# Macaron block on one core: side steps of attention ordered behind the main matmul stream

## The chip, the cores and the metric

The kernel runs on one core of one Trainium2 chip. The metric is the device time of one execution in microseconds (us), lower is better. Three runs of the kernel before took 1823.98 to 1827.08 us, median 1824.61 us.

## The reference, cut to what matters

The input x has 4096 tokens of 256 numbers. It goes through half a feed-forward network, an attention and a second half of the same network, each behind a layer norm:

```python
x = x + 0.5 * ffn(layernorm(x))
x = x + attn(layernorm(x))
x = x + 0.5 * ffn(layernorm(x))
```

The network has a shared part, `silu(x @ sg) * (x @ su) @ sd` with an inner width of 2048, and 8 experts with an inner width of 1024. A router picks two experts for each token, an expert takes at most 640 tokens, and its result is added with the router's weight. Attention works within groups of 64 tokens: q, k, v = x @ w_qkv, q and k pass an RMS norm with weights ln_w, there are 16 heads of 16 numbers, scores are masked causally, and after the softmax comes a product with w_proj. All is float32.

## The kernel before, in words

Every float32 matmul is made of three float16 matmuls: each operand is split into a high part and a low part (high x high, high x low, low x high; `TERMS`, L35). `split` (L102) does this for weights: ScalarE writes the high part (L105), VectorE the low part (L106).

There are four stages (L788 to L817). Stage a does router and shared network of the first half for token blocks 0 to 3; stage b its experts; stage c the shared network of blocks 4 to 7 of the first half, the attention, and the shared network of blocks 0 to 6 of the second half; stage d the experts of the second half and its last shared block. A block is 512 tokens.

The main stream of a shared block (`shared`, L380) runs over 16 chunks of 128 inner columns. For each, `gate_up` (L327) makes two products on TensorE (`pgu`, 6 matmuls of 512 columns each, L337). In stage c the first is followed by tanh on ScalarE (L344) and a VectorE product (L345) that together give silu. After the second, VectorE multiplies both (L350, called the product here), ScalarE casts the high part `hh` (L352) and VectorE subtracts to the low part `hl` (L353). Then `down` (L356) multiplies both by sdw into two PSUM banks `po` (L361, 12 matmuls of 256 columns). The down of a chunk is deferred (`defer`, L97): it is traced after the next chunk's gate and up. After chunk 15 the two banks are evicted into the residual (L394, `xr`) and stored (L397). As its down is deferred, this is traced after the first gate and up of the next block, and the next block's down needs the same two banks. The residual is loaded at chunk 2 (`res_load`, L371). The `pgu` tiles share three PSUM banks; attention and router share three others in stages a and c (`ps_m`, L90).

`shared` yields three times a chunk: after the gate, after the up, after the deferred down. `drive` (L716) mixes the side work in at these points. Every `RATE_C` = 3 main steps it makes one slot of tile steps (`Tiles.steps`, L686) and traces two steps at each following main step, and the rest at the end of the slot; at the end of a block it traces the open slot out. In stage c a side tile is 128 tokens of attention and the next router (`attn_tile`, L507, then `front_steps`, L640, and for each fourth tile `route`, L226), about 27 steps long; a new one starts every `GAP_C` = 4 slots, oldest first within a slot. By steps: load y (L512), stats, normed and cast (L160, L169, L170), transpose by DMA (L179), products `pqk` and `pv` with squares and `vs` (L528 to L541), scaling (L545) and the `QK` copies (L555 to L563), transposes (L567), scores `psc` and mask (L575, L578), maximum and copies of V (L583, L588), exp (L592 to L595), transpose (L598), `py` and `Y` (L606 to L614), a second load of y and the split of Y (L617, L170), transposes (L624), `pao` and the addition (L629, L630), then the norm, transposes and logits of the second half.

What sets the order on each engine: the program is traced in the order above, and then a scheduler orders each engine's queue at build time. It goes through the program with a model of durations, takes from what the model says is ready the instruction that was traced earliest, and so lets a side step overtake the main stream wherever the model finds its input ready. On the chip each queue then runs in that order. `issue_after(ins)` forbids this for a block of code: each of its instructions on the engine of `ins` is queued behind `ins`. It adds no wait. `behind` (L192) applies it to `self.latest`, of which entry 0 is the last ScalarE lookup and entry 1 the last VectorE product. Stage a's tiles are already held so (`Tiles(tile1, 32, GAP_A, n)`, L794); in stage c they are not, and the tanh path of `gate_up` leaves entry 0 as it was.

`attn_init` (L472) runs ahead of stage c's first block. It loads w_qkv in four pieces (L480, one buffer) and w_proj in two pieces of eight loads (L486, one buffer), and splits each piece at once. `fed` (L702) feeds a generator of weights beside a main stream; stage a uses it for the shared weights, once every six main steps.

Of the kernel before, what the change touches and what calls it, by code (L numbers as in the profile page):

```python
# [8 lines left out]
F32 = mybir.dt.float32  # L9
# [5 lines left out]
AF = mybir.ActivationFunctionType  # L15
ALU = mybir.AluOpType
# [4 lines left out]
P = 128  # L21
H = 256
# [3 lines left out]
WS = 16.0  # L26
XP = UP * WS
# [10 lines left out]
class Net:  # L38
# [288 lines left out]
    def gate_up(self, wc, x, h, tanh=False):  # L327

        nc = self.nc
        n = x.shape[-1]  # L330
        ps = []
        for i in range(2):
            p = self.ps_gu.tile([P, n], F32, name="pgu", tag="gu")
            j = 0
            for k in range(2):
                for (w, a) in TERMS:
                    nc.tensor.matmul(  # L337
                        p, lhsT=wc[:, w, i, k, :], rhs=x[:, 2 * a + k, :], start=(j == 0), stop=(j == 5))
                    j += 1
            ps.append(p)  # L340
            if i == 0:
                s = self.hp.tile([P, BT], F32, name="sl", bufs=self.nsl)[:, :n]
                if tanh:
                    nc.scalar.activation(s, p, AF.Tanh, scale=0.5 / XP)  # L344
                    nc.vector.scalar_tensor_tensor(  # L345
                        out=s, in0=s, scalar=1.0, in1=p, op0=ALU.add, op1=ALU.mult)
# [3 lines left out]
        self.latest[1] = nc.vector.scalar_tensor_tensor(  # L350
            out=s, in0=ps[1], scalar=1.0 / XP / (2.0 * XP if tanh else 1.0), in1=s, op0=ALU.mult, op1=ALU.mult).ins
        nc.scalar.copy(h[0], s)  # L352
        nc.vector.tensor_tensor(out=h[1], in0=s, in1=h[0], op=ALU.subtract)  # L353
        yield

    def down(self, outs, nt, h, wd, c, nch):  # L356
# [23 lines left out]
    def shared(self, b, xb, src, dst, tanh=False, late=2):  # L380
        nc = self.nc
        outs = [self.ps_out.tile([P, BT], F32, name="po", tag="po") for _ in range(2)]
        for c in range(16):
            if c == late:
                res = self.res_load(src, b)
            h = [a[:, 0:BT] for a in self.hbuf()]
            yield from self.gate_up(self.sgu[:, c], xb, h, tanh)

            def fin(c=c, h=h):
                self.down(outs, 4, h, self.sdw[:, :, c], c, 16)  # L390
                if c < 15:
                    return
                for i in range(2):
                    nc.vector.scalar_tensor_tensor(  # L394
                        out=res[i], in0=outs[i].rearrange("p (t f) -> p t f", f=H), scalar=0.5 / WS,
                        in1=res[i], op0=ALU.mult, op1=ALU.add)
# [72 lines left out]
            for _ in nxt:  # L469
                pass  # L470

    def attn_init(self, w_qkv, ln_w, w_proj):  # L472
        nc = self.nc
        a = self.at
        self.wqkv = a.tile([P, 2, 2, 3 * H], F16, name="wqkv")
        self.wpr = a.tile([P, 2, 2, H], F16, name="wpr")
        for k in range(2):
            for c0, n in ((0, 2 * H), (2 * H, H)):
                r = a.tile([P, 2 * H], F32, name="rq", tag="q32")[:, :n]
                nc.sync.dma_start(out=r, in_=w_qkv[k * P:(k + 1) * P, c0:c0 + n])  # L480
                self.split(self.wqkv[:, 0, k, c0:c0 + n], self.wqkv[:, 1, k, c0:c0 + n], r)
        wp = w_proj.rearrange("(j r c) f -> r j c f", r=2, c=16)
        for k in range(2):
            r = a.tile([P, H], F32, name="rp", tag="yy")
            for j in range(8):
                nc.sync.dma_start(out=r[j * 16:(j + 1) * 16], in_=wp[k, j])  # L486
            self.split(self.wpr[:, 0, k], self.wpr[:, 1, k], r)
        self.lnw = a.tile([P, H], F32, name="lnw")
        nc.sync.dma_start(out=self.lnw, in_=ln_w.unsqueeze(0).to_broadcast([P, H]))
        self.mask = a.tile([P, 64], F32, name="mask")  # L490
        m2 = self.sm.tile([P, 64], F32, name="m2", bufs=1)
        for m, base in ((self.mask, 0), (m2, -64)):
            nc.gpsimd.memset(m, 0.0)
            nc.gpsimd.affine_select(
                out=m, in_=m, pattern=[[-1, 64]], compare_op=ALU.is_ge, fill=-3.0e38,
                base=base, channel_multiplier=1)
        nc.vector.tensor_copy(self.mask[64:P], m2[64:P])
        self.QK = a.tile([P, 24, P], F16, name="QK")
# [200 lines left out]
        self.slot += 1  # L699


def fed(main, weights):  # L702

    for i, _ in enumerate(main):
        if i % 6 == 0:
            next(weights, None)
        yield

# [27 lines left out]
def macaron(ctx, tc, x, w_qkv, ln_w, w_proj, router_w, rg, ru, rd, sg, su, sd, out):  # L736
    nc = tc.nc
    x = x.rearrange("b s h -> (b s) h")
    out = out.rearrange("b s h -> (b s) h")
    n = Net(ctx, tc)  # L740
    R1 = n.route_init(0)
# [42 lines left out]
    def all_shared(key, b, src, dst, **k):  # L784
        yield from n.shared(b, fbs[key]["xb"], src, dst, **k)
        used.add(key)

    with n.phase("a", BT, 2, 16):  # L788
        n.ident = n.at.tile([P, P], F32, name="ident")
        make_identity(nc, n.ident)  # L790
        weights = n.load_shared(sg, su, sd)
        next(weights)
        n.load_router(router_w)
        tiles = Tiles(tile1, 32, GAP_A, n)  # L794
        run_slots(tiles, ready(1, 0))
# [62 lines left out]
```

## Time and profile before

| | |
|---|---|
| three runs, median (lowest to highest) | 1824.61 us (1823.98 to 1827.08) |
| profiled execution, and its span | 1828.36 us, 1826.6 us |
| TensorE clock granted, mean | 0.998 |
| stage c | about 604 to 1440 us |
| first attention weight split, first `pqk` | 617.5 us, 632.3 us |
| main block ends in stage c, from L394's starts | 682.3, 760.2, 840.7, 921.8, 1002.5, 1083.3, 1164.0, 1244.7, 1318.9, 1388.4 us |
| busy in 720 to 834 us (114 us): PE, DVE, ACT, POOL | 114.0, 89.5, 75.6, 73.4 us |
| busy in 834 to 846 us (12 us): PE, DVE, ACT, POOL | 10.4, 9.5, 8.4, 6.9 us |
| DMA share of 720 to 834, and of 834 to 846 us | 0.67, 0.83 |

PE is TensorE's matmuls, PEld its weight loads, DVE VectorE, ACT ScalarE, POOL GpSimd, SP SyncE, which issues DMAs here. A line of a timeline gives the start in us, the length in us, engine, line, operation, output<-inputs, shapes and how many were merged; in brackets stands how long the engine had been idle before it and what ended that. The waits view sums such idle times by the waiting line and by what ended them. A busy TensorE is not TensorE at its peak, since its matmuls overlap and their ends are modelled.

### The profile page before, as it was taken

To read this page: it belongs to the slowest core of one execution; us is meant where nothing else is said; L and a number is where in the kernel's file an instruction comes from. 1 tells how busy PE (TensorE), PEld (TensorE's weight loads), DVE (VectorE), ACT (ScalarE), POOL (GpSimd) and SP (SyncE) were. 2 spreads that over 40 slices of the span, in tenths; PEclk is the share of its full clock that TensorE was granted. 3 is DMA by queue.
4 is the path that set the end of the run, shared out by engine and by line. 5 is a ranking of instruction groups with operands and counts; after the bars stand their busy time and mean duration, and the time that the engine had idled before them with its cause. 6 is when DMAs were issued, how large, how long until landed. Compare 5 with 4: busy or idle time off the path is not lost.

```text
span 1826.6 us, 37514 instructions
## 1 busy us (share of the span) xinstructions
PE 1778.0 (97%) x13724; PEld 1197.1 (66%) x13724; DVE 1198.9 (66%) x2891; ACT 951.6 (52%) x2055; POOL 754.5 (41%) x1072
## 2 busy tenths in 40 slices
PE   6999999999999899999999999999999999999998
PEld 3555657777777556666666666666655677777765
DVE  6665545666666567787777877887756566666643
ACT  4433334555555466666666666666333455555542
POOL 4666630122111334566767676776430011113210
PEclk9999999999999999999999999999999999999999
DMA  6244132455443356767576776756213144455420
GB/s 196 80 114 114 32 88 63 108 125 120 115 108 87 83 82 99 134 111 148 118 144 118 133 146 117 144 100 130 51 28 73 32 111 108 111 122 122 102 44 12
DMA packets 439193, 185.95 MB, mean 102 GB/s; under 512 B 302305, under 2 KB 436125, under 8 KB 439008
## 3 DMA queue, kind: packets, MB, share of 16 engines
q1 hardware_dynamic: 420528, 161.60, 40.8%
q0 software_dynamic: 17664, 21.17, 6.5%
q8 instruction: 107, 1.75, 0.4%
q10 hardware_dynamic: 816, 0.79, 0.1%
q14 instruction: 78, 0.64, 0.1%
HBM read 78.95 MB, written 42.21 MB: 66 GB/s over the span
## 4 chain that ended last, share of the span: by engine, by line
PE 47%; issue 21%; POOL 12%; DVE 10%; DMA 5%; ACT 3%; SPq 1%; another core or an unknown queue 1%; POOLq 0%; DVEq 0%; ACTq 0%
PE pgu L337 29%; PE po L361 15%; POOL xg L318 3%; DVE sl L350 2%; DMA acc<-eo,eidscatter 2%; DVE sl L345 1%; DVE hl L353 1%; POOL X L316 1%; POOL rstd L150 1%; POOL acc L460 1%; PE pqk L637 1%; POOL S L584 1%; POOL xa L170 1%; ACT sl L344 1%
## 5 line engine op out<-in xcount | busy, mean ns | idle before, releaser
L337 PE MATMUL pgu<-xb,sgu 128*128 128x512 f16 x3072 | 742.2, 380 | 15.5 <-DVE sl L345 8.6
L352 ACT CAST hh<-sl 128x512 f16<-128x512 f32 (+2 forms) x512 | 273.1, 534 | 481.5 <-DVE sl L350 465.5
L337 PE MATMUL pgu<-xe,wc 128*128 128x384 f16 (+1 forms) x3072 | 497.0, 299 | 0.0
L337 PEld LDWEIGHTS <-sgu 128*128 128x128 f16 x3072 | 293.4, 98 | 291.7 <-issue 24.2
L350 DVE SCALAR_TENSOR_TENSOR sl<-pgu,sl 128x512 f32<-128x512 f32 (+2 forms) x512 | 300.7, 588 | 244.8 <-PE pgu L337 213.3
L353 DVE TENSOR_TENSOR hl<-sl,hh 128x512 f16<-128x512 f32 (+2 forms) x512 | 310.8, 607 | 152.6 <-ACT hh L352 147.2
L361 PEld LDWEIGHTS <-hh 128*128 128x128 f16 x3328 | 320.8, 98 | 107.9 <-ACT hh L352 7.3
L337 PEld LDWEIGHTS <-wc 128*128 128x128 f16 x3072 | 300.6, 98 | 92.0
L361 PE MATMUL po<-sdw,hh 128*128 128x256 f16 x2048 | 350.0, 273 | 3.4 <-ACT hh L352 2.2
L361 PE MATMUL po<-sdw,hl 128*128 128x256 f16 x1024 | 247.6, 273 | 6.6 <-DVE hl L353 5.9
L361 PE MATMUL po<-wd,hh 128*128 128x256 f16 x1280 | 223.6, 273 | 0.0
L460 POOL DMA_INDIRECT out_dram<-eo,eidscatter x40 | 65.2, 1629 | 341.5 <-DVE eo L459 331.8
L348 ACT ACTIVATE sl<-pgu 128x384 f32<-128x384 f32 (+1 forms) x336 | 158.9, 473 | 73.0 <-PE pgu L337 43.8
L361 PEld LDWEIGHTS <-hl 128*128 128x128 f16 x1664 | 162.8, 98 | 48.5 <-DVE hl L353 14.7
L460 POOL DMA_INDIRECT acc<-eo,eidscatter x40 | 66.2, 1655 | 293.4 <-DVE eo L459 283.7
L318 POOL DMA_INDIRECT xg<-X,di x128 | 131.3, 1026 | 54.8 <-issue 27.8
L361 PE MATMUL po<-wd,hl 128*128 128x256 f16 x640 | 152.5, 273 | 0.6 <-DVE hl L353 0.6
L345 DVE SCALAR_TENSOR_TENSOR sl<-sl,pgu 128x512 f32<-128x512 f32 x176 | 120.0, 682 | 48.1 <-ACT sl L344 46.9
L344 ACT ACTIVATE sl<-pgu 128x512 f32<-128x512 f32 x176 | 104.2, 593 | 44.9 <-PE pgu L337 35.4
L105 ACT ACTIVATE wc<-re 128x512 f16<-128x512 f32 x128 | 80.5, 629 | 68.9 <-PE pgu L337 59.4
L106 DVE SCALAR_TENSOR_TENSOR wc<-re,wc 128x512 f16<-128x512 f32 x128 | 88.3, 690 | 22.0 <-ACT wc L105 21.8
L584 POOL TENSOR_TENSOR S<-S,amx 128x1024 f32<-128x1024 f32 x32 | 62.1, 1939 | 79.0 <-DVE amx L583 72.0
(150 smaller groups left out, 1713.6 us busy)
## 6 DMA issues: line engine op xcount, KB each, us to landing
re<-in_L_ffn_rg_dram SPq DMA_DIRECT2D x128, 128.0 KB
re<-in_L_ffn_ru_dram SPq DMA_DIRECT2D x128, 128.0 KB
re<-in_L_ffn_rd_dram SPq DMA_DIRECT2D x128, 128.0 KB
y<-acc SPq DMA_DIRECT2D x64, 128.0 KB
y<-in_L_attn_x_dram SPq DMA_DIRECT2D x32, 128.0 KB
acc<-xr SPq DMA_DIRECT2D x16, 256.0 KB
out_dram<-xr SPq DMA_DIRECT2D x16, 256.0 KB
x<-y SPq DMA_DIRECT2D x28, 128.0 KB
```

The source lines that it names most:

```text
L105: nc.scalar.mul(hi, src, WS)
L106: nc.vector.scalar_tensor_tensor(out=lo, in0=src, scalar=WS, in1=hi, op0=ALU.mult, op1=ALU.subtract)
L318: i = nc.gpsimd.indirect_dma_start(out=R["xg"][:, :], out_offset=bass.IndirectOffsetOnAxis(ap=di[:, t, k:k + 1], axis=0), in_=X, in_offset ...
L337: nc.tensor.matmul(p, lhsT=wc[:, w, i, k, :], rhs=x[:, 2 * a + k, :], start=(j == 0), stop=(j == 5))
L344: nc.scalar.activation(s, p, AF.Tanh, scale=0.5 / XP)
L345: nc.vector.scalar_tensor_tensor(out=s, in0=s, scalar=1.0, in1=p, op0=ALU.add, op1=ALU.mult)
L348: self.latest[0] = nc.scalar.activation(s, p, AF.Silu, scale=1.0 / XP).ins
L350: self.latest[1] = nc.vector.scalar_tensor_tensor(out=s, in0=ps[1], scalar=1.0 / XP / (2.0 * XP if tanh else 1.0), in1=s, op0=ALU.mult, op ...
L352: nc.scalar.copy(h[0], s)
L353: nc.vector.tensor_tensor(out=h[1], in0=s, in1=h[0], op=ALU.subtract)
L361: nc.tensor.matmul(o, lhsT=h[a][:, t * P:(t + 1) * P], rhs=wd[:, w], start=(c == 0 and j == 0 and t % 2 == 0), stop=(c == nch - 1 and j == 2),
L460: i = nc.gpsimd.indirect_dma_start(out=R["acc"][:, :], out_offset=bass.IndirectOffsetOnAxis(ap=ids[:, t:t + 1], axis=0), in_=eo, in_offset ...
```

## The change

It has three parts. In stage c the tile steps are now queued behind the latest product and the latest tanh, which the tanh path records. The two evictions of a block are queued behind the low part that was traced last (`self.low`). And attention's weights are no longer loaded and split ahead of the stage, but piece by piece beside its main stream, w_qkv in six pieces; each piece's load is traced two main steps ahead of its split, and the split is queued behind the latest tanh and product.

```diff
@@ gate_up
                 if tanh:
-                    nc.scalar.activation(s, p, AF.Tanh, scale=0.5 / XP)
+                    self.latest[0] = nc.scalar.activation(s, p, AF.Tanh, scale=0.5 / XP).ins
...
-        nc.vector.tensor_tensor(out=h[1], in0=s, in1=h[0], op=ALU.subtract)
+        self.low = nc.vector.tensor_tensor(out=h[1], in0=s, in1=h[0], op=ALU.subtract).ins
@@ shared
                 for i in range(2):
-                    nc.vector.scalar_tensor_tensor(
-                        out=res[i], in0=outs[i].rearrange("p (t f) -> p t f", f=H), scalar=0.5 / WS,
-                        in1=res[i], op0=ALU.mult, op1=ALU.add)
+                    with self.tc.issue_after(self.low):
+                        nc.vector.scalar_tensor_tensor(
+                            out=res[i], in0=outs[i].rearrange("p (t f) -> p t f", f=H), scalar=0.5 / WS,
+                            in1=res[i], op0=ALU.mult, op1=ALU.add)
@@ attn_init, attn_weights
-    def attn_init(self, w_qkv, ln_w, w_proj):
+    def attn_weights(self, w_qkv, w_proj):
...
-            for c0, n in ((0, 2 * H), (2 * H, H)):
-                r = a.tile([P, 2 * H], F32, name="rq", tag="q32")[:, :n]
-                nc.sync.dma_start(out=r, in_=w_qkv[k * P:(k + 1) * P, c0:c0 + n])
-                self.split(self.wqkv[:, 0, k, c0:c0 + n], self.wqkv[:, 1, k, c0:c0 + n], r)
+            for c0 in (0, H, 2 * H):
+                r = a.tile([P, H], F32, name="rq", tag="yy")
+                nc.sync.dma_start(out=r, in_=w_qkv[k * P:(k + 1) * P, c0:c0 + H])
+                yield
+                yield
+                with self.behind(True, 0, 1):
+                    self.split(self.wqkv[:, 0, k, c0:c0 + H], self.wqkv[:, 1, k, c0:c0 + H], r)
...
-            self.split(self.wpr[:, 0, k], self.wpr[:, 1, k], r)
+            yield
+            yield
+            with self.behind(True, 0, 1):
+                self.split(self.wpr[:, 0, k], self.wpr[:, 1, k], r)
+
+    def attn_init(self, ln_w):
+        nc = self.nc
+        a = self.at
+        self.wqkv = a.tile([P, 2, 2, 3 * H], F16, name="wqkv")
+        self.wpr = a.tile([P, 2, 2, H], F16, name="wpr")
@@ fed
-def fed(main, weights):
+def fed(main, weights, every):
...
-        if i % 6 == 0:
+        if i % every == 0:
@@ macaron
-            drive(fed(main, weights) if b == 0 else main, tiles, RATE_A)
+            drive(fed(main, weights, 6) if b == 0 else main, tiles, RATE_A)
...
-        n.attn_init(w_qkv, ln_w, w_proj)
-        tiles = Tiles(tile2, 32, GAP_C)
+        n.attn_init(ln_w)
+        weights = n.attn_weights(w_qkv, w_proj)
+        tiles = Tiles(tile2, 32, GAP_C, n)
         for b in range(NA, NB):
-            drive(all_shared((1, b), b, R1["acc"], R1["acc"], tanh=True), tiles, RATE_C)
+            main = all_shared((1, b), b, R1["acc"], R1["acc"], tanh=True)
+            drive(fed(main, weights, 1), tiles, RATE_C)
```

More of the change, by code (lines that the diff above doesn't have):

```diff
@@ L470, in experts @@
                 pass
-    def attn_init(self, w_qkv, ln_w, w_proj):
+    def attn_weights(self, w_qkv, w_proj):
+        nc = self.nc
+        a = self.at
+        wp = w_proj.rearrange("(j r c) f -> r j c f", r=2, c=16)
+        for k in range(2):
+            for c0 in (0, H, 2 * H):
[5 more added lines that the diff above has]
+                    self.split(self.wqkv[:, 0, k, c0:c0 + H], self.wqkv[:, 1, k, c0:c0 + H], r)
+        for k in range(2):
+            r = a.tile([P, H], F32, name="rp", tag="yy")
+            for j in range(8):
+                nc.sync.dma_start(out=r[j * 16:(j + 1) * 16], in_=wp[k, j])
+            yield
[3 more added lines that the diff above has]
+    def attn_init(self, ln_w):
         nc = self.nc
@@ L476, in attn_init @@
         self.wpr = a.tile([P, 2, 2, H], F16, name="wpr")
-        for k in range(2):
-            for c0, n in ((0, 2 * H), (2 * H, H)):
-                r = a.tile([P, 2 * H], F32, name="rq", tag="q32")[:, :n]
-                nc.sync.dma_start(out=r, in_=w_qkv[k * P:(k + 1) * P, c0:c0 + n])
-                self.split(self.wqkv[:, 0, k, c0:c0 + n], self.wqkv[:, 1, k, c0:c0 + n], r)
[L482 to L486, printed above, removed]
-            self.split(self.wpr[:, 0, k], self.wpr[:, 1, k], r)
         self.lnw = a.tile([P, H], F32, name="lnw")
```

## The prediction

> **What bounds the kernel now.** I read the page first (busy time, then the clock row, 9 in every slice), then TensorE's waits, then the timelines of TensorE, ScalarE and VectorE around the longest waits.
>
> ```profile
> span 1826.6 us, 37514 instructions
> PE 1778.0 (97%) x13724; PEld 1197.1 (66%) x13724; DVE 1198.9 (66%) x2891; ACT 951.6 (52%) x2055; POOL 754.5 (41%) x1072
> ```
>
> TensorE has work nearly always, so only what it waits for can be won, and the change touches stage c (604 to 1440 us) with small side effects in a and d. TensorE's waits in that window (engine and line, what ended the wait, us in total, times, longest):
>
> ```profile
> PE pgu L337 <- DVE sl L345: 8.6, 12, 0.9
> PE po L361 <- DVE hl L353: 5.9, 10, 0.8
> PE pgu L337 <- DVE sl L350: 2.2, 2, 1.5
> PE po L361 <- ACT hh L352: 2.0, 4, 1.0
> ```
>
> With three small rows (0.5, 0.5, 0.3) that is 20.0 us in 31 waits. A 128x512 matmul is shown 0.38 us long, but six in a row take 1.29 us, 0.215 each, so every wait hides another 0.165 us: 20.0 + 31 x 0.165 = 25 us. This is the ceiling for any reordering of stage c. Three quarters of it lies in two places.
>
> Six block ends (838, 919, 1000, 1081, 1162 and 1243 us), all alike. TensorE at the first:
>
> ```profile
> 837.68 1.46 PE L337 MATMUL pgu<-xb,sgu 128*128 128x512 f16 x6
> 840.01 1.45 PE L337 MATMUL pgu<-xb,sgu 128*128 128x512 f16 x6 [0.87 <-DVE sl L345]
> 841.30 0.96 PE L606 MATMUL py<-V,ET 128*128 128x33 f16 x32
> ...
> 843.20 0.28 PE L361 MATMUL po<-sdw,hl 128*128 128x256 f16 x1 [0.71 <-DVE hl L353]
> ```
>
> Two waits, 0.87 + 0.165 = 1.04 and 0.71 + 0.165 = 0.87 us. ScalarE's queue explains the first, VectorE's the second:
>
> ```profile
> 834.66 0.60 ACT L160 ACTIVATE z<-y,nm,rstd 128x256 f32<-128x256 f32 x1 [0.78 <-DVE nm L158]
> ...
> 836.99 0.39 ACT L539 ACTIVATE vs<-pv 128x256 f16<-128x256 f32 x1
> 838.03 0.71 ACT L555 CAST QK<-qk 128x256 f16<-128x256 f32 x2 [0.65 <-DVE qk L545]
> 838.65 0.59 ACT L344 ACTIVATE sl<-pgu 128x512 f32<-128x512 f32 x1
> ```
>
> ```profile
> 839.27 0.69 DVE L345 SCALAR_TENSOR_TENSOR sl<-sl,pgu 128x512 f32<-128x512 f32 x1 [0.55 <-ACT sl L344]
> 840.06 0.69 DVE L350 SCALAR_TENSOR_TENSOR sl<-pgu,sl 128x512 f32<-128x512 f32 x1
> 840.67 0.68 DVE L394 SCALAR_TENSOR_TENSOR xr<-po,xr 128x512 f32<-128x512 f32 x1
> ...
> 841.87 0.68 DVE L394 SCALAR_TENSOR_TENSOR xr<-po,xr 128x512 f32<-128x512 f32 x1
> 842.47 0.68 DVE L353 TENSOR_TENSOR hl<-sl,hh 128x512 f16<-128x512 f32 x1
> ```
>
> The new block's first tanh (L344, at 838.65) stands behind attention's QK copies, which themselves waited 0.65 us for VectorE. The pgu ring has three banks, so the second up product waits until L345 has used that tanh. Then both evictions (L394) stand in front of the low part (L353) that the down matmuls need.
>
> The other place is the start of c (604.6 to 632.4 us): eight waits, 5.1 + 8 x 0.165 = 6.4 us. Two of them (0.39 + 1.54 + 0.33 = 2.3 us, before 609) follow the experts' evictions, which the change doesn't touch. The other 4.2 us come from attention's weight splits, which stop ScalarE in front of main casts:
>
> ```profile
> 617.50 0.63 ACT L105 ACTIVATE wqkv<-rq 128x512 f16<-128x512 f32 x1 [3.93 <-DMA rq<-in_L_attn_w_qkv_dram]
> ...
> 621.00 0.42 ACT L105 ACTIVATE wqkv<-rq 128x256 f16<-128x256 f32 x1 [2.37 <-DMA rq<-in_L_attn_w_qkv_dram]
> ```
>
> **Part 1, tile steps behind the latest product and tanh.** Nothing is added; ScalarE's and VectorE's work of a step may no longer overtake the main stream's last traced tanh and product. Which of the operations ahead of the tanh at 838.65 does that move? A tile starts every 4 slots, a slot is traced over one chunk, and a block's last slot is traced wholly before the next block's first tanh. Counting yields: z, squares, casts and vs are steps of slots 14 and 15 and keep their place. The QK copies belong to slot 16, traced after chunk 1's tanh, and must move behind. The tanh can then follow vs, at 836.99 + 0.39 = 837.4, L345 at 838.0, and the bank is free at 838.7, before TensorE wants it at 838.97. Six waits of 1.04 go: -6.2 us.
>
> What stands late next: the QK copies and L545 run up to a slot later. Their reader, psc, is three slots later, some 15 us at 81 us per block of 16. At the first tiles L545 at 691.8 led to psc at 698.3, 6.5 us, so a slot (5 us) less still covers it. pqk's bank is held until L545, leaving two of three for psc and py; their evacuations follow their own matmuls, which TensorE runs behind the main ones anyway.
>
> The cost is crowding. In every fourth slot the held VectorE work is the row maximum (1.21), Y (4 x 0.29 and two reciprocals of 0.18: 1.5) and L545 (2 x 0.48): 3.7 us, all behind one product now, where it was spread before. With the main three at 0.6 us spacing (1.9) it makes 5.6 us in a chunk that takes TensorE 3.9 + 0.8 for py = 4.7: 0.9 us over. L345 has slack: up, down and gate (1.29 + 1.31 + 1.29 = 3.9) less tanh 0.59 and L345 0.69 is 2.6 us. So the bounds are nothing and 28 tiles x 0.9 = +25 us. Nearer the slack, since the next slot is light: +2.2 us. A gain beyond the six waits is possible at the tile ramp (three waits at 648 to 660, 1.8 us) and is left for the range.
>
> **Part 2, evictions behind low parts.** The same 32 evictions of 0.68 us, now after L353. Behind them on VectorE stand the next L345 and L350; who waits is the next block's first down, which needs the two po banks. From product to the end of the second eviction: 0.69 + 0.62 + 0.68 + 2 x 0.6 and hand-overs, 3.3 us; the first is out at 2.65. With the tanh 1.25 us earlier, the product starts at 838.8 and the banks are free at 841.4 and 842.0. TensorE comes for them at 838.97 + 1.29 + 0.82 (py) = 841.1: a wait of 0.3 to 0.4 for the first bank, none for the second, six matmuls of 0.11 later. So of 0.87 some 0.47 is won, six times: -2.8 us. The ends at 682 and 760 show no such wait today and may get 0.4 each: +0.8. In stage a VectorE is emptier and the first down comes 3.9 us after the first up; evictions done at 3.4 us fit, at no cost. If that cover went, three ends would pay 0.4 each.
>
> One rule speaks against this part. The row of the low parts in 720 to 1260 us (shortest, median, longest ns):
>
> ```profile
> L353 DVE TENSOR_TENSOR hl<-sl,hh x108: 654/692/1236, 721.3 to 1258.7; 128x512 f16<-128x512 f32 x108
> ```
>
> The Trainium skill ("SBUF — State Buffer", section "Who interferes with whom") says that a VectorE instruction with two SBUF inputs is shut out by a GpSimd instruction that reads SBUF until that one ends. The low part is of this kind, the eviction (one PSUM input) is not. By the rule at its worst, an eviction waits out e's 2.14 us on POOL at each of 11 ends: +23 us. By the row the mean is 745 against 692 ns: 11 x 0.05 = 0.6 us. I take the row, inside the 0.4 us above; the longest, 1236, says a single end may lose 0.5.
>
> **Part 3, weights.** Four 128 to 256 KB loads and 4 splits become six loads of 128 KB and 6 splits of 0.42 + 0.42 us; w_proj keeps its 16 small loads (0.42 us of SP each) and 2 splits. ScalarE and VectorE get two instructions and at most 0.4 us more each; behind a split that waits for its data stand the next cast and low part, as today. Each load waits on SP for the split before it, since all share one buffer, and residual and tile loads queue behind; the first pqk comes at 632, eight chunks in, while sixteen calls end within chunk 5. On the chain of waits the loads took 2.1, 2.7 and 4.4 us to the split; two main steps of TensorE give about 2.6. So about half the splits find their data there, and half of the 4.2 us should go: -2.1 us. Bounds: -4.2, and +2 if SP's waits hold up xr or y.
>
> **Sum.** -6.2 - 2.8 + 0.8 - 2.1 + 2.2 = -8.1 us. The profiled execution took 1828.36 us (span 1826.6 and 1.8 around it); 1828.36 - 8.1 = 1820.3. Its median of three is 3.75 us lower: 1824.61 - 8.1 = 1816.5 us.
>
> **Rivals.** *It changes little (1821.5).* The z, squares and vs copies are slow for another reason: z waits for POOL's rstd, and they stay ahead of the tanh. If VectorE is as late without QK, the first wait stays, and half of part 2 and part 3 remain, -3.1 us. For it: 0.78 us of z's wait. Against: the tanh left vs 1.3 us behind.
>
> *Slower (1833).* Crowding decides: the product's queue in every fourth slot pushes L345 past its 2.6 us. It pays from 0.37 us per tile on (10.3 us of gains over 28 tiles); at 0.65 us it costs 18, net +8, 1833; at 0.9, +15, 1840. For it: 5.6 us of VectorE work in 4.7, POOL's blocks on top. Against: VectorE is busy 0.79 of 720 to 834 us, and TensorE there never waited.
>
> **Chances.** Gains as summed, 1808 to 1820.5: 0.58, likeliest 1816.5. Little, 1821 to 1828: 0.16. Crowding, 1829 to 1842: 0.26. A measurement of this kernel tells about 0.2% (3.6 us) from nothing. The range 1808 to 1834 leaves some 0.05 below and 0.13 above.
>
> **What would show it.** Right: the tanh straight behind vs at the six ends, QK copies after chunk 1's tanh, L394 after L353, the pgu row falling from 8.6 us towards 2, po on xr instead of hl at 0.3 to 0.5 each. Wrong: pgu waiting for L345 once every 20 us in mid-block; po waiting on L394 by over 0.9; L105 still waiting 2 us and more before casts; psc or py waiting for transposes.

## The result and the profile after

The changed kernel takes 1838.07 us (median of 6 runs, 1835.36 to 1839.33) where the kernel before takes 1825.45 us (6 runs, 1823.98 to 1827.08): a ratio of 1.0066, interval [1.0055, 1.0076]. It is slower by some 12 us, where 8 us less were forecast, and the time lies outside the range.

The profiled execution took 1838.56 us. The page's first lines after the change (span, then busy time, share and instructions of each engine):

```profile
span 1836.8 us, 37491 instructions
PE 1781.2 (97%) x13724; PEld 1200.2 (65%) x13724; DVE 1237.9 (67%) x2893; ACT 950.6 (52%) x2057; POOL 765.6 (42%) x1072
```

VectorE (DVE) has two instructions more, the two extra splits, and yet is busy 39.0 us longer. Nothing in the change gives it such work, so instructions that were there before have become longer. That line is the first sign of one of the causes.

**Where the time is.** The span grew by 10.2 us. Cut at block evictions, stage a ends 0.2 us earlier (its last block is evicted at 289.0 instead of 289.2 us), b and c together, from there to the last eviction of c, grow from 1158.2 to 1166.9 us, +8.7, and stage d from 374.0 to 375.8. Up to the first gate matmul of c, b takes 309.6 us in both, so the 8.7 us are those of c. Stage d varied between 373.9 and 376.3 us over the kernels below without relation to what was changed in them, so its +1.8 stays open. Within c the loss lies in the six blocks from 760 to 1254 us: the first is 3.5 us longer, the others 0.9 to 1.3 us each (in mid-stage 82.0 instead of 80.7). The three blocks after them gain 0.7 and 2.9 and lose 2.9.

TensorE's waits in stage c after the change (engine and line, what ended the wait, us in total, times, longest). Attention's lines stand 12 further down in the changed kernel: `psc` is L587 for L575, the masking `S` L590 for L578, the scaling L557 for L545.

```profile
PE pgu L337 <- DVE sl L345: 4.0, 9, 1.8
PE po L361 <- DVE hl L353: 3.8, 7, 0.6
PE po L361 <- ACT hh L352: 3.5, 3, 2.0
PE py L618 <- DVE S L590: 2.7, 6, 0.5
PE pgu L337 <- DVE sl L350: 2.6, 2, 1.5
PE psc L587 <- DVE S L590: 2.1, 5, 0.5
PE pl L649 <- DVE vs L552: 1.3, 1, 1.3
PE psc L587 <- DMA QT<-QK: 1.3, 1, 1.3
PE py L618 <- DVE vs L552: 1.2, 6, 0.2
...
```

The two rows at which the change was aimed did fall, from 8.6 to 4.0 and from 5.9 to 3.8 us. Yet the sum rose from 20.0 us in 31 waits to 24.0 in 42. With 0.165 us hidden by each wait that is from 25 to 31 us, +6 of the +8.7; the rest is in no wait that the trace shows. Most of the new time is in side matmuls (`psc`, `py`, `pl`) that want a PSUM bank which VectorE has not yet read out (S is the masking of the scores at L590, `vs` the low part of V at L552): 7.3 us in 18 waits. One waits for a transpose (`QT`) that hasn't landed.

**A block end.** TensorE at the block end that the prediction showed, now 836 to 851 us:

```profile
839.29 0.81 PE L337 MATMUL pgu<-xb,sgu 128*128 128x512 f16 x3
840.55 0.39 PE L587 MATMUL psc<-QT 128*128 128x64 f16 x8 [0.45 <-DVE S L590]
840.78 0.81 PE L337 MATMUL pgu<-xb,sgu 128*128 128x512 f16 x3
841.79 2.75 PE L337 MATMUL pgu<-xb,sgu 128*128 128x512 f16 x12 [0.20 <-DVE sl L345]
...
850.87 0.28 PE L361 MATMUL po<-sdw,hl 128*128 128x256 f16 x1 [0.59 <-DVE hl L353]
```

The wait on L345 is down from 0.87 to 0.20 us and the one on `hl` is gone from its place. But `psc` waits 0.45 us in the middle of the up product, and one chunk later the down waits for a low part after all. ScalarE there:

```profile
839.93 0.60 ACT L160 ACTIVATE z<-y,nm,rstd 128x256 f32<-128x256 f32 x1 [2.63 <-DVE nm L158]
840.44 0.58 ACT L344 ACTIVATE sl<-pgu 128x512 f32<-128x512 f32 x1
```

The evictions start at 843.82 us, straight behind the low part of 843.21, and the `QK` copies are out of the tanh's way, both as meant. Now a `z` stands there, which waits 2.63 us for VectorE's `nm`. It was traced before the tanh, so the hold doesn't move it. `nm` in turn waits for GpSimd's `rstd`, which stands in GpSimd's queue behind the subtraction of e (837.05 to 839.19 us), and the `S` for which `psc` waits stands behind `nm` on VectorE.

The late low part of 850 us shows two effects at once. ScalarE's cast for it, then VectorE, then GpSimd (POOL), in the changed kernel:

```profile
847.12 0.62 ACT L352 CAST hh<-sl 128x512 f16<-128x512 f32 x1 [0.17 <-DVE sl L350]
```

```profile
846.40 0.69 DVE L350 SCALAR_TENSOR_TENSOR sl<-pgu,sl 128x512 f32<-128x512 f32 x1
847.00 1.21 DVE L595 TENSOR_REDUCE amx<-S 128x16 f32<-128x1024 f32 x1
848.13 0.87 DVE L557 SCALAR_TENSOR_TENSOR qk<-pqk,ss,lnw 128x256 f32<-128x256 f32 x2
848.91 0.68 DVE L345 SCALAR_TENSOR_TENSOR sl<-sl,pgu 128x512 f32<-128x512 f32 x1
849.51 0.42 DVE L552 SCALAR_TENSOR_TENSOR vs<-pv,vs 128x256 f16<-128x256 f32 x1
849.84 0.96 DVE L353 TENSOR_TENSOR hl<-sl,hh 128x512 f16<-128x512 f32 x1
```

```profile
848.36 1.90 POOL L596 TENSOR_TENSOR S<-S,amx 128x1024 f32<-128x1024 f32 x1 [5.37 <-DVE amx L595]
850.22 1.75 POOL L568 TENSOR_TENSOR QK<-qk,QK 128x256 f16<-128x256 f32 x2
```

First, VectorE is full: the low part's cast was done at 847.74 us, but it starts 2.1 us later, behind a maximum (L595), a scaling (L557), the next L345 and `vs`, without a gap. This is the crowding of the prediction, at another instruction. Second, the low part itself takes 0.96 instead of 0.69 us: GpSimd's subtraction of the maximum (L596) was reading SBUF until 850.26. L345 and `vs`, which read one operand from PSUM, have their usual lengths in the same stretch. GpSimd in the kernel before, at its block end of 838 us:

```profile
838.71 1.30 POOL L556 TENSOR_TENSOR QK<-qk,QK 128x256 f16<-128x256 f32 x2
839.97 1.16 POOL L562 TENSOR_TENSOR QK<-qk,QK 128x512 f16<-128x512 f32 x1
```

There the `QK` subtractions were over at 841.13, and the low part came at 842.47. The same kind of work, in another order, met nobody.

**One block, wait by wait.** Between its evictions at 843.82 and 925.84 us the changed kernel has five waits of over 0.1 us on TensorE. The down waits 0.59 us for the low part just shown; `py` waits 0.19 us for `vs`, which has a maximum of 1.21 us ahead of it, and 0.45 us for an `S` that stands behind a low part whose cast comes late; `psc` waits 0.46 us for `S` and `pgu` 0.20 us for L345, both by way of the `rstd` behind the subtraction of e. ScalarE ahead of that late cast, copying V straight behind the tanh as the hold orders it:

```profile
904.04 2.49 ACT L600 COPY V<-vs 64x512 f16<-64x512 f16 x4
906.55 0.62 ACT L352 CAST hh<-sl 128x512 f16<-128x512 f32 x1
```

So of these waits only the first has a lengthened low part in it, for 0.27 us. The longest low part of the block costs none, since TensorE was at `pqk` and `pv` meanwhile. VectorE, then GpSimd:

```profile
875.62 2.36 DVE L353 TENSOR_TENSOR hl<-sl,hh 128x512 f16<-128x512 f32 x1
```

```profile
875.30 2.12 POOL L607 TENSOR_TENSOR e<-S,e 128x1024 f16<-128x1024 f32 x1
```

The row of all low parts of 720 to 1260 us, which the prediction had shown with a longest of 1236 ns, is now (shortest, median, longest ns):

```profile
L353 DVE TENSOR_TENSOR hl<-sl,hh x105: 675/693/2564, 723.4 to 1260.0; 128x512 f16<-128x512 f32 x105
```

### The profile page after: what moved, and what is told of

Read it like the earlier page. It is cut to its first block, busy times and chain, and to the rows that moved or that the text cites. A ratio compares the mean times of both kernels' runs of the same rounds, so it can differ in the third digit from the quotient of the medians.

```text
span 1836.8 us, 37491 instructions
## 1 busy us (share of the span) xinstructions
PE 1781.2 (97%) x13724; PEld 1200.2 (65%) x13724; DVE 1237.9 (67%) x2893; ACT 950.6 (52%) x2057; POOL 765.6 (42%) x1072
## 5 line engine op out<-in xcount | busy, mean ns | idle before, releaser
L337 PE MATMUL pgu<-xb,sgu 128*128 128x512 f16 x3072 | 734.5, 380 | 10.9 <-DVE sl L350 5.4
L353 DVE TENSOR_TENSOR hl<-sl,hh 128x512 f16<-128x512 f32 (+2 forms) x512 | 330.8, 646 | 147.5 <-ACT hh L352 145.8
L361 PE MATMUL po<-sdw,hl 128*128 128x256 f16 x1024 | 254.0, 273 | 5.3 <-DVE hl L353 3.8
L345 DVE SCALAR_TENSOR_TENSOR sl<-sl,pgu 128x512 f32<-128x512 f32 x176 | 120.2, 683 | 43.4 <-ACT sl L344 42.6
L596 POOL TENSOR_TENSOR S<-S,amx 128x1024 f32<-128x1024 f32 x32 | 61.3, 1916 | 47.0 <-DVE amx L595 44.0
```

The costliest lines, as they stand in the source:

```text
L337: nc.tensor.matmul(p, lhsT=wc[:, w, i, k, :], rhs=x[:, 2 * a + k, :], start=(j == 0), stop=(j == 5))
L345: nc.vector.scalar_tensor_tensor(out=s, in0=s, scalar=1.0, in1=p, op0=ALU.add, op1=ALU.mult)
L353: self.low = nc.vector.tensor_tensor(out=h[1], in0=s, in1=h[0], op=ALU.subtract).ins
L361: nc.tensor.matmul(o, lhsT=h[a][:, t * P:(t + 1) * P], rhs=wd[:, w], start=(c == 0 and j == 0 and t % 2 == 0), stop=(c == nch - 1 and j == 2),
```

## The experiments

Ratios are to the kernel before, run on the same chip, with 95% intervals; between chips the kernel before itself has medians from 1826 to 1833 us. Edits are against the kernel before where the name begins with "before" or names a part, against the changed kernel where it begins with "after". To count what happens to low parts I took, from the trace, each 128x512 one of 604 to 1440 us (159 in the slowest kernel, 176 in the fastest). It is called blocked when longer than 0.76 us, and its excess is then its length less 0.692 us. Most of it stands beside one instruction: put down to the GpSimd instruction beside which each ran longest, 4.7 of the 9.5 us before (9 low parts) and 19.2 of the 29.0 us after (13) belong to the subtraction of e.

| kernel | ratio | blocked low parts | excess us | longest us |
|---|---|---|---|---|
| before | 1 | 26 | 9.5 | 2.20 |
| low_only | 0.9998 [0.9991, 1.0005] | 26 | 11.4 | 2.21 |
| weights_only | 1.0008 [1.0001, 1.0016] | 28 | 10.7 | 2.20 |
| held_only | 1.0129 [1.0110, 1.0147] | 43 | 39.6 | 2.38 |
| held_low | 1.0051 [1.0038, 1.0065] | 43 | 28.7 | 2.57 |
| after | 1.0066 [1.0055, 1.0076] | 44 | 29.0 | 2.56 |
| after_vs2 | 1.0207 [1.0193, 1.0221] | 60 | 83.7 | 5.37 |
| held_act | 1.0120 [1.0103, 1.0137] | 48 | 52.5 | 2.64 |
| held_dve | 1.0052 [1.0033, 1.0071] | 45 | 46.9 | 3.33 |
| qk_held | 1.0050 [1.0036, 1.0063] | 44 | 32.1 | 2.21 |
| after_free | 1.0316 [1.0302, 1.0330] | 60 | 73.5 | 2.35 |
| before_px, after_px | 0.9976 [0.9967, 0.9984], 1.0013 [1.0005, 1.0021] | 0, 0 | 0 | - |
| before_pp, after_pp | 0.9985 [0.9979, 0.9992], 1.0018 [1.0011, 1.0024] | 0, 0 | 0 | - |
| after_pp_vs2 | 1.0012 [1.0004, 1.0020] | 0 | 0 | - |
| after_pp_free | 0.9989 [0.9982, 0.9995] | 0 | 0 | - |
| before_pp_low | 0.9978 [0.9969, 0.9986] | 0 | 0 | - |

**One part alone.** The first theory was that the hold lets V's copies run so late that `vs`, which has one buffer, and behind it the bank of `pv` stay occupied: from first matmul to last reader that bank is held for some 4 us (median) before and some 13 us after. The rivals were the other two parts.

```diff
 low_only:     +self.low = nc.vector.tensor_tensor(...).ins   and   +with self.tc.issue_after(self.low):  (L394)
 weights_only: attn_weights, attn_init and fed as in the change, and the tanh recorded; Tiles(tile2, 32, GAP_C)
 held_only:    +self.latest[0] = nc.scalar.activation(s, p, AF.Tanh, ...).ins   and   +Tiles(tile2, 32, GAP_C, n)
 after_vs2:    +vs = a.tile([P, 2, H], F16, name="vs", bufs=2)
```

> The kernel before with only the evictions queued behind the low part. Theory (the hold of the tile steps makes the loss, by keeping the PSUM bank of pv from 4.3 to 13.5 us because vs has one buffer): this part alone is harmless, 0.997 to 1.001 of before, the two evictions stand after the low part, and pv's bank is held about 4 us. Rival (late evictions keep the po banks and cost at every block end): 1.003 or more, with waits of po on xr at every block end in stage c.

> The kernel before with only attention's weights loaded and split piecewise beside the main stream (the tanh recorded as latest, tile steps not held, evictions as before). Theory: 0.998 to 1.002 of before; the waits at the start of stage c change by under 3 us and nothing after 640 us. Rival (the split weights hold up SP and shift the tiles, and the loss begins there): 1.004 or more.

> The kernel before with only the tile steps of stage c queued behind the latest product and tanh. Theory: the whole loss is here, 1.005 to 1.010 of before, pv's bank held 13 us or more in the median, TensorE's psc, py and pl waiting for S and vs. Rival (the loss comes from the evictions or the weights): 1.001 or less.

> The changed kernel with two buffers for vs instead of one. Theory: the split of v no longer waits for the held copies of the tile before, pv's bank is held under 6 us, the waits of psc, py and pl on S and vs are gone, and the time falls by 8 to 20 us from the changed kernel, to 0.990 to 1.001 of before. Rival (VectorE is crowded behind the product, so that buffers don't matter): within 0.2% of the changed kernel, 1.005 or more of before, with the waits on S and L345 in place.

The first three put the loss on the hold: alone it costs 1.29%, more than the 0.5 to 1.0% expected, the others 0.08% at most. low_only did what its part says, but for less. TensorE at a block end:

```profile
844.35 1.46 PE L337 MATMUL pgu<-xb,sgu 128*128 128x512 f16 x6 [0.87 <-DVE sl L345]
...
847.22 0.38 PE L361 MATMUL po<-sdw,hh 128*128 128x256 f16 x2 [0.61 <-DVE xr L395]
```

The first wait is untouched, and the second is now for the evictions, 0.61 + 0.165 = 0.78 against 0.87 us: 0.1 us per end, not 0.47. In weights_only ScalarE still stops at the pieces:

```profile
624.39 0.42 ACT L105 ACTIVATE wqkv<-rq 128x256 f16<-128x256 f32 x1 [5.15 <-DMA rq<-in_L_attn_w_qkv_dram]
624.71 0.60 ACT L352 CAST hh<-sl 128x512 f16<-128x512 f32 x1
628.51 0.42 ACT L105 ACTIVATE wqkv<-rq 128x256 f16<-128x256 f32 x1 [3.20 <-DMA rq<-in_L_attn_w_qkv_dram]
```

The cast behind the first piece is late, and TensorE waits 1.8 us for it, so that one such wait takes the place of several.

after_vs2 killed the theory. `pv`'s bank is held only some 5 us there, and the kernel became much slower, 1.0207. Its longest waits are for low parts. GpSimd, VectorE and TensorE of after_vs2 at 1003 us:

```profile
1003.20 0.98 POOL L318 DMA_INDIRECT xg<-X,di  x1 [0.30 <-issue]
1004.18 1.93 POOL L596 TENSOR_TENSOR S<-S,amx 128x1024 f32<-128x1024 f32 x1
1006.04 1.31 POOL L568 TENSOR_TENSOR QK<-qk,QK 128x256 f16<-128x256 f32 x2
1007.30 1.16 POOL L574 TENSOR_TENSOR QK<-qk,QK 128x512 f16<-128x512 f32 x1
1008.39 0.66 POOL L316 COPY X<-tokid 128x1 f32<-128x1 f32 x1
```

```profile
1003.66 5.35 DVE L353 TENSOR_TENSOR hl<-sl,hh 128x512 f16<-128x512 f32 x1
```

```profile
1009.07 0.40 PE L361 MATMUL po<-sdw,hl 128*128 128x256 f16 x1 [3.00 <-DVE hl L353]
```

A subtraction of 0.69 us stood for 5.35 us while GpSimd ran one instruction after another, first the issue of an indirect DMA and then SBUF readers, and TensorE lost 3.00 us. The second theory follows: the hold moves the copies that feed GpSimd to just behind the main stream's tanh and product, so that GpSimd's subtractions start just when the low part wants its two SBUF operands. What share of the loss this is has to be tested.

**Low parts that can't be blocked.** The theory is tested by giving the low part only one SBUF operand. In px it reads the up product from PSUM instead of `sl` (this leaves silu out of the low part, so only its time is of use); in pp the product is written back to its PSUM bank, and cast and low part read it there. Both change stage c's tanh path only. With another operand the scheduler prices the instruction otherwise, so a pair's queues differ: matched by name and count over stage c, 344 of 1496 VectorE instructions stand elsewhere in before_pp than in before, 318 of 1498 in after_pp than in after, and 174 of 1498 in after_pp_vs2 than in after_vs2.

```diff
 px: -tensor_tensor(out=h[1], in0=s, in1=h[0], op=ALU.subtract)
     +scalar_tensor_tensor(out=h[1], in0=ps[1], scalar=1.0 / XP, in1=h[0], op0=ALU.mult, op1=ALU.subtract)
 pp: +o = ps[1] if tanh else s
     -product: out=s;  nc.scalar.copy(h[0], s);  tensor_tensor(out=h[1], in0=s, in1=h[0])
     +product: out=o;  nc.scalar.copy(h[0], o);  tensor_tensor(out=h[1], in0=o, in1=h[0])
```

> The kernel before, but in stage c the low part is taken from the up product in PSUM and the high part, so that it has one SBUF operand instead of two (the low part's values are then not those of the reference; its cost is meant to be the same 0.68 us). Theory (GpSimd's reads shut the low part out, and the hold makes that happen more often): low parts over 0.76 us fall from 26 to 3 or fewer, the time to 0.995 to 1.000 of before. Rival (the loss comes from side banks held longer by the order alone): 0.998 to 1.003.

> The changed kernel with the same low part (one SBUF operand, values not those of the reference). Theory: the low parts' 29 us of excess vanish, the time is at most 1.002 of the kernel before with this low part, so most of the loss of 0.7% is gone. Rival (banks): it stays 1.005 or more above the kernel before with this low part, with TensorE waiting for S and vs as it does in the changed kernel.

> The kernel before with the product of stage c written back into its PSUM bank, so that cast and low part read it there: the low part has one SBUF operand and all values are the reference's. Theory (GpSimd shuts out two-operand low parts): no low part over 0.76 us, 0.996 to 0.999 of before, as with the low part taken from the up product (0.9976). Rival (that gain came from a shuffled order): 1.000 to 1.004.

> The changed kernel with the same product in PSUM. Theory (two causes: shut-out low parts, and tile chains so late that transposes are waited for): the first is gone, the second stays: 1.000 to 1.003 of before, TensorE's waits on S and vs under 3 us, those on the transposes of e 4 us or more. Rival (shut-out low parts are all of it): at most 1.001 of the kernel before with the product in PSUM. Rival (they are none of it): 1.005 or more of before.

The row of the low parts in after_pp:

```profile
L354 DVE TENSOR_TENSOR hl<-pgu,hh x173: 649/692/694, 612.3 to 1439.1; 128x512 f16<-128x512 f32 x173
```

The longest of 173 is 694 ns, and that is not for want of company: 48 of them began while a GpSimd instruction had at least another 0.2 us to run, 63 of 172 in the changed kernel, whose 44 blocked ones all ran beside GpSimd. In after_pp_free it is 80 of 175, none lengthened, in after_free (below) 82 of 159, with 60 blocked. So it is the second SBUF operand, and not the order alone, that lets GpSimd lengthen a low part. The page's busy time of VectorE falls to 1188.1 us, from 1237.9 in the changed kernel and 1198.9 before. In pp the cast also takes 0.586 instead of 0.618 us; in px it doesn't, with no less gain.

By the total time the change now costs 1.0013/0.9976 = 1.0037 in one pair and 1.0018/0.9985 = 1.0033 in the other, half of the 1.0066. This puts after_px between its two readings (at most 1.002, and 1.005 or more), and it is not the blocked low parts alone, since the orders of a pair differ too. In the profiled executions, one of each kernel, stage c from its first gate matmul to its last eviction is 8.7 us longer after than before, 6.5 us in the pp pair and 5.4 us in the px pair. So a quarter to a half of the loss goes with the low part's operand; the rest is something else. TensorE's waits in after_pp point to it:

```profile
...
PE py L619 <- DMA ET<-e: 3.8, 5, 1.6
...
PE py L619 <- DVE vs L553: 2.9, 6, 0.5
PE pao L650 <- DVE vs L553: 1.9, 5, 0.5
PE psc L588 <- DMA QT<-QK: 0.8, 3, 0.4
```

Transposes land after their readers want them, and banks still come free late (4.8 us on `vs`, where under 3 were expected; before_pp has none of it, and 0.6 us on `ET`). From the issue of a tile's second transpose `QT` to `psc` there were 13.3 us (median of 32 tiles; least 6.8) before, 6.5 us (least 3.2) in after_pp; from the issue of `ET` to `py` at least 6.2 us before and 4.3 in after_pp.

**Which held work does it.** held_act and held_dve hold tile steps on one engine only. qk_held holds nothing but the `QK` copies, the only operations whose move the prediction had wanted.

```diff
 held_act:  self.held.behind(..., 0)        held_dve:  self.held.behind(..., 1)
 held_low:  held_only, and the evictions behind the low part
 qk_held:   +with self.behind(True, 0):   around the QK copies (L549 to L563), the tanh recorded, Tiles not held
```

> Only ScalarE's part of the hold in stage c (behind the latest tanh), nothing else of the change. If the copies of V that keep vs's only buffer are the cause (banks), the loss is here: 1.008 or more of before, pv's bank held 12 us or more. If low parts shut out by GpSimd are the cause, the time goes with their excess: under 1.005 if that stays below 25 us.

> Only VectorE's part of the hold in stage c (behind the latest product), nothing else of the change. If held V copies are the cause: 1.003 or less, pv's bank held under 7 us. If low parts shut out by GpSimd are the cause, the maximum and the scaling of q and k now start GpSimd's S and QK subtractions just ahead of the low part: excess above 25 us and 1.006 or more.

> The hold in stage c together with the evictions behind the low part, without the piecewise weights. The hold alone gave 1.0129, the whole change 1.0066, while evictions and weights alone gave 0.9998 and 1.0008. If the evictions' place decides at block ends where the next low part meets GpSimd: 1.005 to 1.008, low parts' excess about 29 us. If the weights do (they shift the tiles): 1.011 or more, excess about 40 us.

> The kernel before with only the QK copies of ScalarE queued behind the latest tanh. The first step of the prediction by itself: at six block ends the tanh follows vs and the wait of 1.04 us on L345 goes, -6 us. Theory: the wait goes, but GpSimd's QK subtractions, which follow these copies, now meet more low parts: 0.997 to 1.002. Rival (the hold is harmful wherever it is put): 1.005 or more.

held_act keeps nearly the whole loss. Its time allows both readings, as `pv`'s bank is held some 14 us there; its first row of waits is the low part:

```profile
PE po L361 <- DVE hl L353: 15.3, 12, 2.0
```

That fits GpSimd: 39.2 of its 52.5 us of excess stand beside the subtraction of e, which follows a cast of ScalarE. held_dve, at 1.0052, lies between its two readings (1.003 or less, 1.006 or more), and TensorE's waits there are mostly for transposes (`ET` 12.2 us, `QT` 5.2). qk_held was expected near no change and missed: 1.0050 is the figure of its rival. The first wait at the block ends did go, but the low parts' excess beside `QK` rose from 3.3 to 17.1 us and beside e from 4.7 to 13.6, and `ET` became late, at each of the six block ends:

```profile
PE py L607 <- DMA ET<-e: 7.7, 7, 1.6
```

held_low shows that the parts are not additive: the evictions behind the low parts do nothing alone, but take held_only from 1.0129 to 1.0051, with an excess of 28.7 instead of 39.6 us. The subtraction of S lengthens 7 low parts by 8.4 us in held_only, all within 9 us of a block end, and none in held_low; that of e costs 25.0 us against 19.2.

**The rest, and a better kernel.** "Free" lets two tile steps, the scaling with the `QK` copies and the exp, run without the hold, so that their transposes start earlier. before_pp_low is the kernel before with pp and the evictions behind the low parts.

```diff
 free: yields ahead of the scaling step and of the exp step: -yield  +yield "free"
       Tiles.steps: a step after "free" runs without self.held.behind(...)
```

> The changed kernel with the product in PSUM and two buffers for vs. Without shut-out low parts 0.33% of loss is left (1.0018 against 0.9985). If that rest comes from pv's bank, held 13 us for vs's only buffer: pv's bank under 7 us, no waits on vs, 0.999 to 1.000 of before. If it comes from late tile chains: 1.001 to 1.005, the waits on transposes still there or longer.

> The changed kernel with the product in PSUM, and two of a tile's steps let out of the hold: scaling with the QK copies, and the exponential with its split. Both feed transposes. If the rest of the loss comes from late tile chains: the waits on transposes go, 0.998 to 1.000 of before. If it comes from pv's bank: 1.0015 or more, with the waits on vs in place.

> The kernel before with the product in PSUM and the evictions behind the low part, no hold and no split weights. The low part is no longer shut out, so the evictions behind it can't be delayed by it: 0.997 to 0.9985 of before if the late eviction then helps at block ends, 0.9985 to 1.000 if the po banks are then waited for as in the run of this part alone.

> The changed kernel with only the two transposing steps (scaling with the QK copies, exponential with its split) let out of the hold; the low part keeps its two SBUF operands. If late tile chains and shut-out low parts are separate costs, only the first goes: about 1.004 of before, low parts' excess still near 29 us. If the two steps' GpSimd subtractions are also what shuts the low parts out, both go: at most 1.001 of before, excess under 15 us.

after_pp_free takes 0.9989. The times from `QT` to `psc` are back at 12.7 us (least 7.3), no transpose wait for `QT` or `ET` is left, and its rows are down to:

```profile
PE po L362 <- ACT hh L353: 3.6, 4, 1.9
PE pgu L337 <- DVE sl L345: 3.4, 6, 2.1
PE po L362 <- DVE xr L396: 2.8, 6, 0.8
...
```

What is left of the hold then costs 0.9989 against 0.9985, nothing that can be told. A second `vs` buffer (after_pp_vs2) changes nothing beyond the intervals: the waits on `vs` are gone, but those on `QT` grew from 0.8 to 6.9 us. That a long-held `pv` bank, my first theory, need not cost anything is shown by after_pp_free, where it is still held some 13 us (median). The same second buffer that cost 1.4% without pp is harmless with it.

after_free, meant as the other corner, missed both readings: freeing the two steps without pp gives 1.0316, the slowest of all. Its low parts are blocked 60 times, and the banks that VectorE empties are late. Two of TensorE's rows, and VectorE ahead of one such wait:

```profile
PE psc L587 <- DVE qk L557: 21.5, 18, 1.8
PE pl L649 <- DVE vs L552: 11.0, 6, 1.8
```

```profile
988.02 0.88 DVE L557 SCALAR_TENSOR_TENSOR qk<-pqk,ss,lnw 128x256 f32<-128x256 f32 x2 [1.27 <-POOL ss L547]
```

The second row fits the blocked VectorE: at 910 us a low part of 2.11 us stands ahead of `vs`. The first does not: ahead of each of these waits the freed scaling had VectorE idle for 0.8 to 2.0 us, until GpSimd's `ss` came, and no long low part was near. In after_pp_free VectorE idles as long for `ss` (38.6 us in stage c, against 38.2), yet both rows are gone and the time is 0.9989; 165 of 1498 VectorE instructions also stand elsewhere there. How much of the 3.3% is the operand's doing is not shown. The earlier statement must be bounded: freeing the steps gained only in the kernel in which low parts can't be blocked.

before_pp_low is the fastest kernel with the reference's values, 0.9978, some 4 us below before and 16 below the change. Against before_pp (0.9985) the intervals overlap, so the evictions' own share is not shown.

## Why the prediction was wrong, by its steps

Three costs of part 1 were put at little or nothing: GpSimd's lengthening of VectorE's instructions, the crowding in front of the low part, and side banks that are read out late. Which of them costs how much of the 8.7 us is not shown.

**"Nothing is added" (part 1) and "I take the row" (part 2).** These two failed, and they are one mistake. The rule of the Trainium skill ("SBUF — State Buffer", section "Who interferes with whom") was set against the row of the low parts before, and only for the evictions' part. The row was measured in the old order. What decides the blocking is where GpSimd's instructions lie against the low part, and part 1 changes just that. The same section also says that issue order decides who blocks, and this was the part to read: a reordering can't be costed at the row of the old order. The prediction put 0.6 us by the row and 23 us by the rule; measured, the excess went from 9.5 to 29.0 us, +19.5, and a quarter to a half of the loss went with the low part's second SBUF operand. The view itself was cut too narrowly: over all of stage c the low parts before already had one of 2.2 us, where the window shown ended at 1.24. That this case follows the rule is shown by the low parts that never exceed 694 ns once an operand is in PSUM, though GpSimd still runs beside them.

**"Still covers it".** The 6.5 us joined two tiles: the scaling of 691.8 us has its `psc` at 717.8. From scaling to `psc` there are 19.9 us (median; least 12.5) before and 13.7 (least 11.4) after, so for `QK` the cover nearly held: one wait of 1.3 us in the changed kernel. What was not counted is the transpose of e, which is held too: in after_pp `ET` is waited for 3.8 us. Freeing both steps takes 1.0018 to 0.9989. Of the 0.66% the order pp, then free, assigns 0.33 to pp, 0.29 to the freed steps, and 0.04 to nothing that can be told. The prediction's own sign for this ("psc or py waiting for transposes") did appear.

**"Six waits of 1.04 go".** Right in place, less in size: the first wait fell from 1.04 to 0.36 us at five of the six ends and went at the sixth, and the second went from its place at all six. It didn't pay, because a wait of `psc` (0.26 to 0.46 us at five ends) and one for a low part in the next chunk (0.53 to 0.60 us at all six) came instead: at the first end 1.7 us with the hidden time, where it had been 1.9. The tanh does not follow `vs`; a `z` that waits for `rstd` came between, which the rival "It changes little" had named.

**"pqk's bank is held until L545 ... their evacuations follow their own matmuls".** This put no cost on side banks. After the change `S` and `vs` end waits that did not exist, 7.3 us in 18, because these two stand late in VectorE's queue: behind a maximum, behind a low part whose cast is late, or behind a norm that waits for GpSimd. after_free, where `pqk`'s bank waits for a scaling that waits for GpSimd, shows the sizes that this can reach.

**Crowding, +2.2 us, and the rival "Slower (1833)".** The mechanism was right, the place and the size were not. Crowding was weighed against the slack of L345 alone, and the row of `pgu` waiting for L345 fell from 8.6 to 4.0. It shows at the low part instead, which at 850 us comes 2.1 us after its cast is done, and on ScalarE, where four copies of V (2.49 us) stand ahead of a cast. A block's five waits then make 1.89 + 5 x 0.165 = 2.7 us, where the two of a block in mid-stage made 1.9. The rival had VectorE, and it named "POOL's blocks on top", though without a figure for them; its size range (1833 to 1840) holds the result, in part by luck.

**Parts 2 and 3.** -2.8 +0.8 was measured at 0.9998 [0.9991, 1.0005], with 0.1 us won per end. -2.1 was 1.0008 [1.0001, 1.0016]: counted from the same point of stage c (604 to 640 us before, 609.8 to 645.8 in weights_only), the waits went from 5.1 us in 8 to 5.3 in 5. "About half the splits find their data there" held in weights_only, where five of eight splits waited 0.55 us or less, but not for the piece that counts, the first (5.15 us).

**What stays open.** The excess doesn't fix the time: held_dve has 46.9 us and 1.0052, held_act 52.5 us and 1.0120, after_vs2 83.7 and 1.0207, after_free 73.5 and 1.0316. Where in a chunk a low part is blocked, and what stands behind it, must matter (at 875.62 us 2.36 us cost TensorE no wait); no run separates that. No run moves only the low part's operand in a fixed order, so the quarter to a half given above holds the change of order too, and how the loss divides between blocked low parts, crowding and late tile steps stays open.

## What to carry to other kernels

Before work is moved, list for each moved step what it sets off on GpSimd, and which VectorE instructions with two SBUF operands will then run beside it; a duration row from before holds only for the order from before. If a critical VectorE instruction can take one operand from PSUM, do that first: here the kernels with it lie from 0.9976 to 1.0018, and their partners without it from 0.9998 to 1.0316. When work is queued behind an instruction, look at what it will then stand in front of: here the slack of L345 was counted and that of the low part was not. And where waits for PSUM banks appear, look at what stands ahead of the evacuation in its engine's queue, and what that waits for, before blaming the banks.

## What the hardware showed that was not expected

- One low part can be shut out by several GpSimd instructions in a row: 5.35 us, from 1003.66 to 1009.01, beside the issue of an indirect DMA until 1004.18, a subtraction of 1.93 us, three more that ended at 1008.46, and a copy. In the other kernels with two SBUF operands the longest was 2.2 to 3.3 us.
- Small VectorE instructions suffer too, one with a single input tile among them: `ss` [128x2] took 1.89 us or more instead of 0.17 at six block ends of the changed kernel, beside the subtraction of e. Over stage c all VectorE instructions that ran over 10% longer than their median in both kernels together had some 28 us of excess before and 61 after, of which the low parts are 9.5 and 29.0; most of the rest after are `ss` and router sums of [128x8]. ScalarE's instructions had 1.0 to 1.7 us over their medians in any kernel.
- GpSimd is lengthened in turn: at 850.22 us the first of the two `QK` subtractions took 1.12 us beside the low part, where in the kernel before two took 1.30 together.
